# A diffusion-transformer block on one core: takes of k and loads of x tied to VectorE's place, one more tile normed in the projection, the last output tiles stored in quarters

## The chip, the core and the metric

The kernel runs on one core of a Trainium2 chip. The core has five engines that work beside each other, each with its own queue of instructions: TensorE (PE: matmuls; the loading of its weights is listed apart as PEld), VectorE (DVE), ScalarE (ACT), GpSimd (POOL) and SyncE (SP, here only a queue for data transfers). A transfer (DMA) is issued from the queue of SP, ACT or POOL and then moves data by itself. The engines wait for each other only through semaphores. The metric is the time of one execution in microseconds on the device; less is better.

## The reference

Two sequences of 2048 tokens with 576 features go through one transformer block whose norms are modulated by a condition:

```python
mod = silu(c) @ w_ada + b_ada
sh_msa, sc_msa, g_msa, sh_mlp, sc_mlp, g_mlp = split(mod, 6, axis=1)
xn = ln(x) * (1 + sc_msa) + sh_msa
q, k, v = split_heads(xn @ w_qkv + b_qkv)      # 16 heads of 36
q, k = ln(q) * qn_g + qn_b, ln(k) * kn_g + kn_b
o = softmax(q @ k.T * 36**-0.5) @ v
x = x + g_msa * (o @ w_proj + b_proj)
xn2 = ln(x) * (1 + sc_mlp) + sh_mlp
x = x + g_mlp * (gelu(xn2 @ w1 + b1) @ w2 + b2)   # 576 -> 2304 -> 576
```

All is in float32.

## The kernel before

The kernel first tests on the device whether the norms' gains and biases are small (then softmax needs no maximum) and branches. With the reference's inputs `block_of_small` runs, and the rest of this section is about it.

**Stages.** For each of the two sequences ("blocks", b = 0, 1): `inputs` norms 16 tiles of 128 tokens, multiplies them with w_qkv, norms the heads and lays q and k out by feature in two large tiles, qo (features 0 to 639) and kr (640 to 1151). `attend` then does the attention, and `outputs` the projection with the residual. After both blocks comes the MLP in two halves: the first product with GELU, whose results go to DRAM, and the second product, `second_product`, which reads them back for 256 tokens at a time (q = 0 to 15) and stores the output. Both halves of the MLP use Strassen's scheme with seven products in the place of eight.

**The attention.** The 16 heads are worked in 8 pairs p; each pair has 4 blocks qb of 512 queries, and each of these 4 groups g of keys. A step (p, qb, g) computes scores (L981), exponentials on ACT (L985) and, one step behind, the products with v (L994). DVE copies the first group's result into a tile ot (L1040) and adds the next three (L1042). There are two ot tiles. When the fourth group is in, `finish` sends the row of sums through DRAM to be spread over 64 partitions (den, L1009 and L1010), and three steps later `divided` takes the reciprocal, multiplies, and stores the result with SP's queue from ot into qo (L1019), where the q of the same pair lay. Only then is this ot tile free.

Scores need q and k at certain partitions. They are brought there by transfers within the on-chip memory: `take_q(p, qb)` brings 512 queries into qm (main dims) and qe (the last four dims of each head, four times), 8 to 10 transfers on SP's queue, asked for one qb ahead; `take_k(p)` brings all keys of a pair into km[p % 2] and ke[p % 2], 8 to 10 transfers on POOL's queue, asked for at step (p - 1, 1, 1). What a take returns (`parted`, on DVE) is run some steps later: the list `later` holds work by the number of steps that it is put off.

**The residual.** Beside the attention, `residual_begun(b, t)` prepares x + bias: it loads tile t of x into spare[t % 2], adds the bias to tile t - 1 on POOL, and stores it to x1_dram. The spare tiles lie in kr, in keys that are no longer needed. It is hooked to step (3 + t // 4, t % 4, 3), t = 0 to 16.

**What sets the order.** TensorE's instructions run in the order of the program throughout. In the attention, DVE's and POOL's do too (a manual schedule). A fixed order is not a fixed time: an engine runs ahead in its queue as far as its semaphores let it. POOL's instructions in the attention are takes of k and the residual; a take of k waits for nothing but the last scores that read its tile, those of the pair two before. ACT's and SP's order is set by the framework's planner, which also puts some later transfers of POOL (L1085, loads of x1 for the projection) among the attention's.

**The projection of block 1.** `outputs` calls `placed(t)` at each of 16 places t; `between` holds what is done there. For the MLP's first block of 512 tokens (four tiles i) it is: load the tile with ACT's queue (place 2i + 5), norm it (2i + 7, DVE with a square root on ACT), transpose it on TensorE and modulate it on ACT (2i + 8). In the MLP, `ahead(job)` does the same for the next block's tiles, with POOL's queue: load at a job three before, norm one before, four transposes (L1393) one behind and the fifth two behind. For tile (1, 0), which is wanted at the very start, the load stands before the first job and the norm in job 0. ACT's first instruction of the MLP is the copy of a product into cs (L1360). The rows' tiles xt go round: five of them in the attention and the projection, three in the MLP.

**The end.** In `second_product` the seven products come as pairs (3, 4), (2, 5), (6, 7) and (1,). DVE combines them into c00, c01, c10, c11, the quarters of y for two tiles of 128 tokens, multiplies by the gate (L1505), adds the residual xr (L1506), and POOL's queue stores each tile (L1507).

Of the kernel before, what the change touches and what calls it, by code (L numbers as in the profile page):

```python
# [8 lines left out]
F32 = mybir.dt.float32  # L9
# [3 lines left out]
ALU = mybir.AluOpType  # L13
# [3 lines left out]
P = 128  # L17
# [14 lines left out]
def dit_block(  # L32
# [25 lines left out]
    nc = tc.nc  # L58
# [6 lines left out]
    HALF = C // 2  # L65
    BLK = 512
    NBLK = N // BLK
    TPB = BLK // P
# [71 lines left out]
    with tc.tile_pool(name="bound", bufs=1, side="right") as bound:  # L140
# [11 lines left out]
        product = bound.tile([1, 1], F32, name="product")  # L152
# [129 lines left out]
    with psum_pools(), tc.tile_pool(name="ada", bufs=2) as ada:  # L282
# [11 lines left out]
        for i, ins in enumerate(((qn_g, kn_g), (qn_b, kn_b))):  # L294
# [3 lines left out]
            out=gb_rows, in_=rows_dram.rearrange("i w h d -> (i w h d)").rearrange("(c p) -> c p", p=P)  # L298
# [53 lines left out]
    def modulated(dst, src, which, b, apart=False):  # L352

        t4, t1 = transposed(*src, apart)
        for k in range(NKC):
            nc.scalar.activation(  # L356
                dst[:, k, :],
                t4[:, k * P : (k + 1) * P] if k < FULL else t1[:, :P],
                AF.Identity,
                bias=mod[:, which, k, b : b + 1],  # L360
                scale=mod[:, which + 1, k, b : b + 1],
            )
# [353 lines left out]
    def block_of_small():  # L716
# [13 lines left out]
        kv, close_kv = opened("kv")  # L730
# [9 lines left out]
        for t in (*ke, *qe):  # L740
            nc.gpsimd.memset(t, 0.0)
        high = kv.tile([P, BLK], F32R, name="high")

        low_k, low_q, sign_k, sign_q = (kv.tile([P, 1], F32, name=f"part{i}") for i in range(4))
        parts = ident.rearrange("p (r a b) -> p r a b", a=2, b=2)
# [35 lines left out]

        def take_k(p):
            m, e = km[p % 2], ke[p % 2]
            src = lambda c: slice(c * N // 2, (c + 1) * N // 2)
            rows_taken(nc.gpsimd, m, e, range(2), C + p * 2 * HD, src, slice(0, N // 2))
            return lambda: parted(e, slice(0, P), low_k, sign_k)
# [39 lines left out]
        def tile_normed(xt):  # L826
            return rows_normed(xs["pool"], xt)
# [235 lines left out]
        spare = [kr[:, c, a * 640 : a * 640 + C] for c in range(4) for a in range(3)]  # L1063

        def residual_begun(b, t):

            if t == 0:
                nc.gpsimd.dma_start(out=spare[2], in_=gate_dram[1, b, :].partition_broadcast(P))
            if t < NT:
                nc.gpsimd.dma_start(out=spare[t % 2], in_=x[b, t * P : (t + 1) * P, :])  # L1070
            if t > 0:
                rows = spare[(t - 1) % 2]
                nc.gpsimd.tensor_tensor(rows, rows, spare[2], ALU.add)
                nc.gpsimd.dma_start(out=x1_dram[b, (t - 1) * P : t * P, :], in_=rows)
# [160 lines left out]
        NB = B * NBLK  # L1235
        NPART = BLK // PAIR
        gelus = [dram.tile([NPART, P, NF, PAIR], F32, name=f"gelu{n}") for n in range(NB)]
        mx, close_mx = opened("mx")
        xnts = [mx.tile([P, NKC, BLK], F32, name=f"xnt{i}") for i in range(2)]
# [22 lines left out]
        def mlp_loaded(n, i, queue):  # L1262
            b, blk = divmod(n, NBLK)
            t0 = blk * BLK + i * P
            return tile_loaded(x1_dram[b, t0 : t0 + P, :], queue)

        first, between = {}, {}
        for i in range(TPB):
            cols = slice(i * P, (i + 1) * P)
            between.setdefault(2 * i + 8, []).append(  # L1270
                lambda i=i, cols=cols: modulated(xnts[0][:, :, cols], first[i], 2, 0)
            )
            between.setdefault(2 * i + 5, []).append(lambda i=i: first.update({i: mlp_loaded(0, i, nc.scalar)}))
            between.setdefault(2 * i + 7, []).append(lambda i=i: first.update({i: tile_normed(first[i])}))
        for i, t in enumerate((6, 8, 10, 12, 14)):
            between.setdefault(t, []).append(weight_sums[i])
        in_order = tc.manual_schedule(engines={mybir.EngineType.DVE})
# [97 lines left out]
        def ahead(job):  # L1375


            n, f = divmod(job, HF)

            def at(offset):  # L1380
                m, g = divmod(job - offset, HF)
                return (m + 1, g // 2) if m + 1 < NB and g % 2 == 0 and g // 2 < TPB else None

            if todo := at(-3):
                rows_ahead[todo] = mlp_loaded(*todo, nc.gpsimd)
            if todo := (1, 0) if job == 0 else at(-1):
                rows_ahead[todo] = tile_normed(rows_ahead[todo])
            for offset, chunks in ((1, range(FULL)), (2, (FULL,))):
                if todo := at(offset):
                    m, i = todo  # L1390
                    src, tail = rows_ahead[todo] if offset == 1 else rows_ahead.pop(todo)
                    for k in chunks:
                        nc.tensor.transpose(  # L1393
                            ps_t[:, k % FULL * P : (k % FULL + 1) * P],
                            src[:, k * P : (k + 1) * P] if k < FULL else tail,
                            ident,
                        )
                    for k in chunks:
                        nc.scalar.activation(
                            xnts[m % 2][:, k, i * P : (i + 1) * P],  # L1400
                            ps_t[:, k % FULL * P : (k % FULL + 1) * P],
                            AF.Identity,
                            bias=mod[:, 2, k, m // NBLK : m // NBLK + 1],
                            scale=mod[:, 3, k, m // NBLK : m // NBLK + 1],
                        )
# [14 lines left out]
            nc.sync.dma_start(out=hidden[q % len(hidden)], in_=gelus[n][g])  # L1420

        rows_ahead = {}
        for i in range(2):
            rows_ahead[1, i] = mlp_loaded(1, i, nc.gpsimd)
        token_sums(0)
        for job in range(0, NB * HF, 2):
            (n0, f0), (n1, f1) = divmod(job, HF), divmod(job + 1, HF)
# [26 lines left out]
        def second_product(q, gate, gate_bias):  # L1454

            b, t0 = divmod(q * PAIR, N)
            ht = hidden[q % len(hidden)]

            def part(t, k):
                return ht[:, k * HF : (k + 1) * HF, t * P : (t + 1) * P]  # L1460

            stationary = {3: part(0, 0), 4: part(1, 1)}
            for m, x_, y_, op in (
                (2, part(1, 0), part(1, 1), ALU.add),
                (5, part(0, 0), part(0, 1), ALU.add),
                (6, part(1, 0), part(0, 0), ALU.subtract),
                (7, part(0, 1), part(1, 1), ALU.subtract),
                (1, part(0, 0), part(1, 1), ALU.add),
            ):
                stationary[m] = hs.tile([P, HF, P], F32, name=f"as{m}")  # L1470
                nc.vector.tensor_tensor(stationary[m], x_, y_, op)  # L1471
            xr = []
            for t in range(2):
                xr.append(hs.tile([P, C], F32, name="xr", bufs=2))
                nc.sync.dma_start(out=xr[t], in_=x1_dram[b, t0 + t * P : t0 + (t + 1) * P, :])
                nc.gpsimd.tensor_tensor(xr[t], xr[t], gate_bias, ALU.add)
            y = [hs.tile([P, 2, HALF], F32, name="y", bufs=3) for _ in range(2)]
            c00, c01, c10, c11 = y[0][:, 0, :], y[0][:, 1, :], y[1][:, 0, :], y[1][:, 1, :]
            ms = {}
            for pair in ((3, 4), (2, 5), (6, 7), (1,)):  # L1480
                ps = s_tile()
                for a, m in enumerate(pair):
                    ms[m] = ps[:, a, :HALF]
                    for f in range(HF):
                        nc.tensor.matmul(  # L1485
                            ms[m], stationary[m][:, f, :], ws[m][:, f, :], start=(f == 0), stop=(f == HF - 1)
                        )
                if pair == (3, 4):
                    nc.vector.tensor_copy(c01, ms[3])
                    nc.vector.tensor_copy(c10, ms[4])  # L1490
                elif pair == (2, 5):
                    nc.vector.tensor_tensor(c00, c10, ms[5], ALU.subtract)
                    nc.vector.tensor_tensor(c11, c01, ms[2], ALU.subtract)
                    nc.vector.tensor_tensor(c10, c10, ms[2], ALU.add)
                    nc.vector.tensor_tensor(c01, c01, ms[5], ALU.add)
                elif pair == (6, 7):
                    nc.vector.tensor_tensor(c11, c11, ms[6], ALU.add)
                    nc.vector.tensor_tensor(c00, c00, ms[7], ALU.add)
            if q + 3 < NB * NPART:
                hidden_loaded(q + 3)  # L1500
            nc.vector.tensor_tensor(c00, ms[1], c00, ALU.add)
            nc.vector.tensor_tensor(c11, ms[1], c11, ALU.add)
            for t in range(2):
                rows = y[t].rearrange("p a f -> p (a f)")
                nc.vector.tensor_tensor(rows, rows, gate, ALU.mult)  # L1505
                nc.vector.tensor_tensor(rows, rows, xr[t], ALU.add)  # L1506
                nc.gpsimd.dma_start(out=out[b, t0 + t * P : t0 + (t + 1) * P, :], in_=rows)  # L1507
# [49 lines left out]
```

## Time and profile before

| | |
|---|---|
| median of 3 runs | 3247.49 us (3244.83 to 3251.32) |
| the profiled execution | 3251.16 us, of which the span from the first to the last instruction is 3249.3 us |
| TensorE's granted clock | 0.997 of full speed |

Stages by the trace, with the busy time of the engines in them:

| stage | from | to | PE | DVE | ACT | POOL |
|---|---|---|---|---|---|---|
| attention, block 0 | 256 | 1050 | 791.80 | 287.15 | 534.15 | 84.85 |
| projection, block 0 | 1050 | 1122 | 71.59 | 26.50 | 1.86 | 10.28 |
| inputs, block 1 | 1122 | 1366 | 244.00 | 159.06 | 81.50 | 33.77 |
| attention, block 1 | 1366 | 2140 | 772.49 | 270.18 | 529.59 | 74.84 |
| projection, block 1 | 2140 | 2214 | 74.00 | 42.58 | 9.59 | 17.14 |
| MLP, first product | 2214 | 2746 | 529.14 | 259.80 | 256.82 | 14.54 |
| MLP, second product | 2746 | 3235 | 489.00 | 244.79 | 1.77 | 78.04 |
| end | 3235 | 3250 | 0.04 | 3.67 | 0.00 | 1.10 |

How to read the profile's lines: L12 is line 12 of the kernel, `out<-in` are tiles by their names in the program, `xN` is how many instructions are merged in a row. A timeline row has start and duration in microseconds, the instruction, and in brackets how long its engine had been idle and what ended that. A chain row has start, duration and what the end of the kernel was waiting for at that time. A q behind an engine's name (SPq) means its sequencer, which waits, branches and issues. An instruction that issues a transfer is listed with the time of the issue; the data land later.

### The profile page before, as it was taken

Reading aid. Unit: us, or ns where it says so; the run is one execution under the profiler, and the core shown is the slowest. Engines: PE = TensorE matmul, PEld = TensorE weight load, DVE = VectorE, ACT = ScalarE, POOL = GpSimd, SP = SyncE. Lnnn points to the kernel's source line nnn. Section 1 sums busy time; section 2 is a strip of 40 time slices with the busy share of each in tenths; the row PEclk is TensorE's granted clock in tenths of the full one; section 3 lists DMA queues with packets and bytes.
Section 4 is the critical chain, followed back from the end, with each engine's and each line's share of the span. In section 5 each row is a group of like instructions: output and inputs, shape, how many; then the busy total and the mean of one; then the engine's idle time right before and its main releaser. Section 6 shows DMA issues by size and latency. Waiting matters only on the chain.

```text
span 3249.3 us, 46887 instructions
## 1 busy us (share of the span) xinstructions
PE 3212.6 (99%) x18143; PEld 1884.8 (58%) x18143; DVE 1450.2 (45%) x2073; ACT 1496.4 (46%) x2950; POOL 354.1 (11%) x435
## 2 busy tenths in 40 slices
PE   8999999999999999999999999999999999999998
PEld 5775333333333777633333333367888888777776
DVE  4664333333333366633333333345555443455454
ACT  2335666666666033366666666623555542000000
POOL 1111000012200111100011110010000000111111
PEclk9999999999999999999999999999999999999999
DMA  4112222233311411121223222154322223333321
GB/s 130 26 25 65 76 51 61 74 77 85 93 33 34 144 26 27 25 54 44 51 71 75 59 55 66 33 181 149 119 90 94 87 84 127 135 125 113 116 99 38
DMA packets 127795, 253.15 MB, mean 78 GB/s; under 512 B 22915, under 2 KB 65868, under 8 KB 125516
## 3 DMA queue, kind: packets, MB, share of 16 engines
q1 hardware_dynamic: 103956, 181.48, 18.3%
q0 software_dynamic: 22880, 67.11, 7.5%
q8 instruction: 145, 2.38, 0.3%
q10 hardware_dynamic: 728, 1.48, 0.2%
q14 instruction: 86, 0.70, 0.1%
HBM read 135.40 MB, written 66.35 MB: 62 GB/s over the span
## 4 chain that ended last, share of the span: by engine, by line
PE 95%; issue 2%; DMA 1%; DVE 1%; POOL 0%; SPq 0%; ACT 0%; DVEq 0%; POOLq 0%; ACTq 0%
PE b L994 28%; PE b L981 19%; PE s L370 14%; PE s L1485 14%; PE m L1334 12%; PE m L1348 2%; PE s L381 2%; PE one L1334 2%; PE s L884 1%; PE t L1393 0%; PE s L348 0%; DMA wq<-in_w_qkv_dram 0%; DMA qo<-ot 0%; DMA wa<-in_w_ada_dram 0%; PE b L192 0%
## 5 line engine op out<-in xcount | busy, mean ns | idle before, releaser
L985 ACT ACTIVATE pt<-b 128x512 f32<-128x512 f32 x2048 | 1058.0, 608 | 493.4 <-PE b L994 276.8
L994 PE MATMUL b<-pt,vt 128*64 128x512 f32 x4096 | 936.7, 599 | 0.0
L994 PEld LDWEIGHTS b<-pt,vt 128*64 128x64 f32 x4096 | 272.1, 137 | 582.8 <-issue 441.3
L981 PE MATMUL b<-qm,km 32*128 32x512 f32 x4096 | 570.7, 614 | 3.3 <-DVE ot L1040 2.5
L981 PE MATMUL b<-qe,ke 16*128 16x512 f32 x2048 | 424.3, 788 | 0.0
L1042 DVE TENSOR_TENSOR ot<-b,ot 128x512 f32<-128x512 f32 x192 | 132.8, 692 | 650.3 <-PE b L994 649.8
L370 PE MATMUL s<-wq,xnt 128*128 128x288 f32 x1536 | 392.8, 411 | 1.6 <-DMA wq<-in_w_qkv_dram 1.6
L981 PEld LDWEIGHTS b<-qm,km 32*128 32x128 f32 x4096 | 192.8, 185 | 275.5 <-ACT pt L985 206.9
L1485 PE MATMUL s<-ws,as 128*128 128x288 f32 x1440 | 351.8, 406 | 0.0
L370 PEld LDWEIGHTS s<-wq,xnt 128*128 128x128 f32 x1536 | 286.3, 191 | 93.3 <-issue 18.5
L1485 PEld LDWEIGHTS s<-ws,as 128*128 128x128 f32 x1440 | 273.6, 190 | 75.6
L1013 DVE RECIPROCAL den<-den 128x512 f32<-128x512 f32 x64 | 214.0, 3343 | 11.7 <-DMA den<-den_dram 11.7
L1334 PE MATMUL m<-xnt,wb 128*128 128x256 f32 x864 | 214.0, 384 | 0.0
L1334 PE MATMUL m<-s,wb 128*128 128x256 f32 x864 | 210.1, 379 | 0.2 <-DVE s L1304 0.2
L1040 DVE COPY ot<-b 128x512 f32<-128x512 f32 x64 | 44.3, 692 | 343.7 <-PE b L994 315.7
L1334 PEld LDWEIGHTS m<-xnt,wb 128*128 128x128 f32 x864 | 159.2, 190 | 32.5 <-issue 12.2
L1334 PEld LDWEIGHTS m<-s,wb 128*128 128x128 f32 x864 | 164.1, 190 | 22.9 <-DVE s L1304 0.6
L981 PEld LDWEIGHTS b<-qe,ke 16*128 16x128 f32 x2048 | 108.7, 184 | 114.7 <-issue 113.0
L1361 DVE TENSOR_TENSOR cs<-m,cs 128x512 f32<-128x512 f32 x72 | 49.7, 691 | 215.6 <-ACT cs L1360 154.0
L1485 PE MATMUL s<-ws,hidden 128*128 128x288 f32 x576 | 142.3, 406 | 0.0
L356 ACT ACTIVATE xnt<-s,mod 128x128 f32<-128x128 f32 x180 | 66.8, 460 | 160.2 <-PE s L349 146.3
L1471 DVE TENSOR_TENSOR as<-hidden 128x1152 f32<-128x1152 f32 x80 | 139.0, 1801 | 0.0
(162 smaller groups left out, 2550.0 us busy)
## 6 DMA issues: line engine op xcount, KB each, us to landing
gelu<-cs SPq DMA_DIRECT2D x144, 256.0 KB
hidden<-gelu SPq DMA_DIRECT2D x16, 2304.0 KB
den<-den_dram SPq DMA_DIRECT2D x128, 128.0 KB
x_dram<-kr POOLq DMA_DIRECT2D x48, 288.0 KB, 3.3
qm<-qo SPq DMA_DIRECT2D x192, 64.0 KB
kr<-in_x_dram POOLq DMA_DIRECT2D x32, 288.0 KB, 3.8
xr<-x_dram SPq DMA_DIRECT2D x32, 288.0 KB
out_dram<-y POOLq DMA_DIRECT2D x32, 288.0 KB, 3.8
```

The source lines that it names most:

```text
L356: nc.scalar.activation(dst[:, k, :], t4[:, k * P : (k + 1) * P] if k < FULL else t1[:, :P], AF.Identity, bias=mod[:, which, k, b : b + 1], ...
L370: nc.tensor.matmul(outs[a], stationary(k, a), moving(k, a), start=(first and k == 0), stop=(not first and k == FULL - 1),)
L381: nc.tensor.matmul(outs[a], stationary(FULL, a)[r], moving(FULL, a)[r], start=first, stop=not first)
L981: nc.tensor.matmul(ps, k[r, keys], q[r, :], start=first, stop=not first)
L985: nc.scalar.activation(pt[:, h, :], banks[2 * c + h], AF.Exp, scale=SCALE)
L994: nc.tensor.matmul(acc[64 * h : 64 * h + 64, :], vt[:, v0 : v0 + 64], pt[:, h, :], start=pt is pts[0][0], stop=pt is pts[-1][0],)
L1013: nc.vector.reciprocal(den, den)
L1042: nc.vector.tensor_tensor(ot, acc, ot, ALU.add)
L1334: nc.tensor.matmul(out_m[m], wb[:, slot[m], k, f * P : (f + 1) * P], moving[m](k), start=k == 0 and (m == 1 or (first and m in (2, 5, 6))) ...
L1348: nc.tensor.matmul(out_m[m], w[r, f * P : (f + 1) * P], a[r, FULL, t * PAIR : (t + 1) * PAIR], start=first and m != 4, stop=not first and ...
L1471: nc.vector.tensor_tensor(stationary[m], x_, y_, op)
L1485: nc.tensor.matmul(ms[m], stationary[m][:, f, :], ws[m][:, f, :], start=(f == 0), stop=(f == HF - 1))
```

## The change

Three parts. First, a helper `not_sooner(tile)` copies one element of a tile on DVE. It stands ahead of the transfers of `take_k(p)` for p > 2 (one copy for each of the two tiles) and ahead of each load of x in `residual_begun`. A transfer that overwrites the element must come after the copy, and DVE comes to the copy in the order of the program; so POOL can't issue these transfers before DVE has reached this place.

Second, the work on tile (1, 0), the first of the MLP's second block, moves from the MLP's start into block 1's projection, so that five tiles are loaded, normed and modulated there. All places of these five are two earlier than before. In the MLP, its load, its norm in job 0 and its transposes in jobs 1 and 2 are gone.

Third, in the last call of `second_product`, each quarter of the output is multiplied by the gate and given the residual as soon as its sums are complete but for the last product, and is stored by itself with SP's queue: two quarters behind pair (2, 5), and two at the end, where the last product is multiplied by the gate (in the tile xr, which is free by then) and added.

```diff
+        met = kv.tile([1, 1], F32, name="met")
+        def not_sooner(there):
+            nc.vector.tensor_copy(met, there[0:1, 0:1])
...
         def take_k(p):
             m, e = km[p % 2], ke[p % 2]
+            if p > 2:
+                not_sooner(m)
+                not_sooner(e)
...
             if t < NT:
+                not_sooner(spare[t % 2])
                 nc.gpsimd.dma_start(out=spare[t % 2], in_=x[b, t * P : (t + 1) * P, :])
...
-        for i in range(TPB):
-            cols = slice(i * P, (i + 1) * P)
-            between.setdefault(2 * i + 8, []).append(
-                lambda i=i, cols=cols: modulated(xnts[0][:, :, cols], first[i], 2, 0)
+        for j in range(TPB + 1):
+            n, i = divmod(j, TPB)
+            to = xnts[n][:, :, i * P : (i + 1) * P]
+            between.setdefault(2 * j + 6, []).append(lambda j=j, to=to: modulated(to, first[j], 2, 0))
+            between.setdefault(2 * j + 3, []).append(
+                lambda j=j, n=n, i=i: first.update({j: mlp_loaded(n, i, nc.scalar)})
             )
-            between.setdefault(2 * i + 5, []).append(lambda i=i: first.update({i: mlp_loaded(0, i, nc.scalar)}))
-            between.setdefault(2 * i + 7, []).append(lambda i=i: first.update({i: tile_normed(first[i])}))
+            between.setdefault(2 * j + 5, []).append(lambda j=j: first.update({j: tile_normed(first[j])}))
...
-                return (m + 1, g // 2) if m + 1 < NB and g % 2 == 0 and g // 2 < TPB else None
+                there = m + 1 < NB and g % 2 == 0 and g // 2 < TPB and (m, g) > (0, 0)
+                return (m + 1, g // 2) if there else None
...
-            if todo := (1, 0) if job == 0 else at(-1):
+            if todo := at(-1):
...
-        for i in range(2):
-            rows_ahead[1, i] = mlp_loaded(1, i, nc.gpsimd)
+        rows_ahead[1, 1] = mlp_loaded(1, 1, nc.gpsimd)
...
+            last = q == NB * NPART - 1
...
+            def half_stored(t, n):
+                nc.sync.dma_start(out=half(out[b, t0 + t * P : t0 + (t + 1) * P, :], n), in_=y[t][:, n, :])
...
+                if last and len(pair) == 2 and pair != (3, 4):
+                    for t in range(2):
+                        n = 1 - t if pair == (2, 5) else t
+                        part = y[t][:, n, :]
+                        nc.vector.tensor_tensor(part, part, half(gate, n), ALU.mult)
+                        nc.vector.tensor_tensor(part, part, half(xr[t], n), ALU.add)
+                        if pair == (2, 5):
+                            half_stored(t, n)
+            if last:
+                for t in range(2):
+                    product = half(xr[t], t)
+                    nc.vector.tensor_tensor(product, ms[1], half(gate, t), ALU.mult)
+                    nc.vector.tensor_tensor(y[t][:, t, :], y[t][:, t, :], product, ALU.add)
+                    half_stored(t, t)
+                return
```

More of the change, by code (lines that the diff above doesn't have):

```diff
@@ L1479, in second_product, with half @@
             ms = {}
+            def half(ap, n):
+                return ap[:, n * HALF : (n + 1) * HALF]
+            def half_stored(t, n):
+                nc.sync.dma_start(out=half(out[b, t0 + t * P : t0 + (t + 1) * P, :], n), in_=y[t][:, n, :])
             for pair in ((3, 4), (2, 5), (6, 7), (1,)):
```

## The prediction

> **What bounds the kernel now.** I read the page from the top: first the engines' busy shares, then the chain that ended last, then the list of waits of TensorE, and last the stretches where one of these waits sits.
>
> ```profile
> PE 3212.6 (99%) x18143; PEld 1884.8 (58%) x18143; DVE 1450.2 (45%) x2073; ACT 1496.4 (46%) x2950; POOL 354.1 (11%) x435
> ...
> PE 95%; issue 2%; DMA 1%; DVE 1%; POOL 0%; SPq 0%; ACT 0%; DVEq 0%; POOLq 0%; ACTq 0%
> ```
>
> TensorE is busy 99% of the span and is 95% of the chain. The change takes no matmul away, so it can gain only where TensorE stands still, and at the ends of the kernel. Its waits in the middle are few:
>
> ```profile
> PE t L1393 <- DVE xt L278: 2.7, 1, 2.7
> PE b L981 <- DVE ot L1040: 2.5, 2, 1.4
> ```
>
> The columns are microseconds in total, times, longest. The second row understates the loss, because a late start also spreads the matmuls behind it. I therefore take the distance between the starts of successive L994 runs (one step of attention each) from the chain of waits around the wait in pair 3 of block 0:
>
> ```profile
> 566.52 3.58 PE b L994 x16
> ...
> 572.50 1.03 PE b L994 x4
> ...
> 574.97 3.78 DMA qo<-ot
> ...
> 580.97 3.58 PE b L994 x16
> ...
> 586.95 3.58 PE b L994 x16
> ```
>
> A step takes 5.98 us (572.50 - 566.52; 586.95 - 580.97), and the stalled one 8.47: lost 2.49. The same chain around 1663 in block 1 has starts at 1657.08, 1663.06, 1671.30, 1678.97: 2.26 + 1.69 lost. Two more lost steps are in block 0, 766.38 to 773.02 (0.66) and 862.70 to 869.12 (0.44). All four places end with DVE's copy of a sum into ot (L1040) waiting for the store qo<-ot that still reads that buffer. **Sum 7.5 us.**
>
> Why is that store late? It stands on SyncE's queue behind the takes of q. In the timeline of SyncE's queue, the stalled place and then the next, undisturbed one:
>
> ```profile
> 560.32 4.75 SPq L764 DMA_DIRECT2D qm<-qo  x4
> 565.12 6.28 SPq L767 DMA_DIRECT2D qe<-qo  x3
> 571.45 1.83 SPq L764 DMA_DIRECT2D qm<-qo  x2
> 573.38 0.67 SPq L767 DMA_DIRECT2D qe<-qo  x1
> 574.15 1.56 SPq L1019 DMA_DIRECT2D qo<-ot  x2
> ...
> 586.73 2.84 SPq L764 DMA_DIRECT2D qm<-qo  x4
> ```
>
> Ten takes need 13.7 us (560.32 to 574.05) where they need 7.7 at 586.73 (to 594.40). Beside the first ones run the eight takes of k, which POOL issued from 560.58 on, when TensorE ended the pair before: its queue runs ahead to the start of every pair, where SyncE is busiest.
>
> **The change, part by part.**
>
> *Ties (take_k of pairs 3 to 7, residual_begun).* Added are 5 x 2 x 2 + 16 x 2 = 52 copies of one element on DVE. No such row exists; the nearest, the reciprocal of 128x1 (L277), takes 0.16 us: 8.3 us in all, on an engine that is busy 287 of 794 us in the first attention, so nothing on the path. What they wait for: k's main and end tiles were written a whole pair earlier; the residual's tile was last written by POOL's addition one hook earlier, some 24 us (four steps) before. So I cost the wait at 0. If POOL came later than that, behind the copy stand the sums into ot, and TensorE waits for these.
>
> The takes of k now start behind DVE's sum of step (p, 1, 0). In the undisturbed place that sum is at 596.55 to 597.24, while the takes of q ended at 594.40 and the qo<-ot store was issued by 596.83. So the eight takes (4.5 us of POOL's issue, 0.5 to 0.6 each, 6.3 us to landing) run from about 597.5 to 609, and the next takes of q start at 610.64. Beside them is only the exchange of the sums (den), whose reader, the reciprocal, comes three steps (18 us) later. The parting of k on DVE stands four steps (24 us) behind, against 11 us for the takes. Hidden. At pair starts the takes of q then need their 5.4 or 7.5 us, and the store comes 4 us before its reader (its last packet in the trace at 598.2, L1040 at 602.53). Gain: the whole **7.5 us**; ends: 0 if the takes stay slow, and a loss in the rival below.
>
> The residual's load and store (288 KB each) move from bursts at pair starts to one pair at each fourth step, about 4.5 us behind the start of a take of q. [...] The POOL addition now lies beside DVE's reciprocal; at 783.23 they lay together and it took its usual 3.34.
>
> *Tile (1, 0) normed in the projection.* Moved are one load (from POOL, 0.54, to ACT's queue, 0.33 to 0.36), one norm (DVE 2.2 from 2173.22 to 2175.41, ACT 0.5), five transposes (0.66 + 0.27 of PE, equal before and after) and five modulations (ACT 1.86). The chain of waits at the start of the MLP shows what goes:
>
> ```profile
> 2221.94 0.04 ACT cs L1360
> ...
> 2222.74 0.59 DVE xt L278
> ...
> 2223.37 0.66 PE t L1393 x4
> ```
>
> ACT was held at its copy cs (L1360) until 2221.94 and its sqrt stood behind, so TensorE waited 2.7 us for the norm. Without these transposes its next work (L1348, 3.4 us, then some 7 us) needs nothing of ACT; the sums of DVE that free the bank end near 2226.5, TensorE needs the bank near 2231. Late next is nothing. In the projection all norms come two places earlier. The new first one meets DVE idle (6.39 us before 2167.04) and ends near 2162, 6 us before TensorE wants it at 2168.4. The load's data are block 0's, written long before; the other four loads were issued at 1282.9 to 1325.5, the fifth follows tile 15's transposes near 1345, where ACT has 0.9 us idle. **-2.7 us**, ends 0 and -3.0.
>
> *The last tiles.* The last matmul ends near 3235.1. Behind it now come two additions, four operations of 576 columns and POOL's stores:
>
> ```profile
> 3235.08 0.46 DVE L1501 TENSOR_TENSOR y<-s,y 128x288 f32<-128x288 f32 x1 [3.55 <-PE s L1485]
> ...
> 3239.26 0.55 POOL L1507 DMA_DIRECT2D out_dram<-y  x1 [0.98 <-DVE y L1506]
> ```
>
> The program's last line, by engine and kind (count, ns min/median/max, first and last start):
>
> ```profile
> L1553 SPq EVENT_SEMAPHORE  x14: 17/28/28, 3212.2 to 3249.2; - x14
> ...
> L1553 POOLq DRAIN  x3: 46/98/6514, 3241.9 to 3249.0; - x3
> ```
>
> POOL's drain begins at 3241.9, before the last store landed (3242.06), and lasts 6.51 us; the span ends 0.8 us behind it. So not the store, but POOL's drain sets the end. In the change POOL's last work is the addition to xr, which ended at 3214.7, so its drain can lie beside the matmuls. Then the end is: four DVE operations of 288 columns (0.46 + 0.53 + 0.37 + 0.45, with 0.1 for the wait between dependent ones): 3237.0; SyncE's issue 0.36: 3237.4; its branch to the last line, 3.4 us (before: branch 3208.8, first wait 3212.2); ten waits of 0.06; the closing 0.8: about 3242.2. That is **-7.1 us**. The four new operations behind each of the pairs (2, 5) and (6, 7), 4 x 0.37 = 1.5 us, lie beside 8.7 and 4.4 us of matmuls.
>
> [...] The drain's price in the new place no row shows. Ends: if it always follows the last store, only the earlier issue is won (3239.8 to 3237.4, -2.4); if free, -7.1. I take -7.1, since ACT's drain (2755.7) and PE's (3234.0) ran as soon as these engines were through.
>
> **Sum:** 7.5 + 2.7 + 7.1 = 17.3. The profiled execution took 3251.16 (span 3249.3), so it would be 3233.9; the median of the runs shown is 3247.49 (3244.83 to 3251.32), 3.7 below: **3230**.
>
> **Rivals.**
> A. The drain stays at the end: 17.3 - 4.7 = 12.6, 3235. For it: the drain outlasts the last landing by 6.4. Against: it didn't wait to begin.
> B. The takes of q stay slow at pair starts (then k's takes were not the cause), attention keeps its 7.5: 9.8, 3238. Against: 7.3 to 7.7 in every undisturbed place. That the tie does not hold POOL back ends here too.
> C. Both: 5.1, 3242.
> D. Slower: k's takes and the residual now press on the qo<-ot store, which is in flight just when they start. It has 4.3 us from last packet to reader; once its landing (1.4 us beside nothing, 3.0 beside the residual at 575.7) passes 5.7, L1040 waits and TensorE with it. At the price of the stall of pair 3, 2.5 us, at ten places (pairs 2 to 6, two blocks): +25 against 9.8 won, about 3263. For it: k's takes nearly doubled the takes of q. Against: their first packets come 1 us after the issue, when the store is mostly through.
>
> **Chances:** forecast 0.60 (its own range 3225 to 3234), A 0.11, B 0.07, C 0.09, D 0.13. No change is within 0.2%, 6.5 us, about what a measurement can tell. Faster: forecast, A, B: 0.78. Same: C: 0.09. Slower: D: 0.13. The range, 3225 to 3243, takes in A to C and leaves D out.
>
> **What would show it.** Right: no L1040 waiting for qo<-ot; ten takes in 7 to 8 us at every pair start; POOL's km rows of pairs 3 to 7 some 37 us later in the pair; no row L1393 <- DVE; POOL's drain before 3225, the end some 7 us behind the last matmul. Wrong: DVE copies that wait for POOL, L994 steps over 6 us at (p, 1, 0) (D), a 6.5 us drain at the end (A).

## The result and the profile after

| | before | after |
|---|---|---|
| median | 3247.49 us (3244.83 to 3251.32) | 3231.15 us (3230.51 to 3231.41) |
| profiled execution | 3251.16, span 3249.3 | 3230.51, span 3228.7 |

The ratio of the times is 0.9950, interval 0.9935 to 0.9964: 16.3 us less by the medians, where 17.3 were forecast, and 20.6 us less between the two profiled spans. The kernel has also become steadier: its runs lie within 0.9 us of each other, those of before within 6.5. In all that follows, a time is compared with that of the kernel before in the same session (3247.5 to 3249.2).

Line numbers of after are higher by 6 to 35: L990 are the scores, L1003 the products with v, L1049 and L1051 the copy and the sums into ot, L770 and L773 the takes, L1028 the store qo<-ot. The busy shares, the shares of the chain that ended last, and the list of TensorE's waits on the page and trace of after:

```profile
PE 3206.4 (99%) x18143; PEld 1883.0 (58%) x18143; DVE 1450.4 (45%) x2131; ACT 1495.7 (46%) x2950; POOL 353.5 (11%) x432
...
PE 99%; DMA 1%; DVE 0%; SPq 0%; issue 0%; ACT 0%; DVEq 0%
```

```profile
PE s L370 <- DMA wq<-in_w_qkv_dram: 2.5, 1, 2.5
PE s L370 <- DVE ot L1051: 0.8, 1, 0.8
...
PE m L1345 <- DVE s L1315: 0.2, 1, 0.2
```

TensorE's share of the chain went from 95% to 99%. Neither the 2.7 us for the norm in the MLP nor a wait for ot's copy is left among its waits; those shown, and one of 10.6 us for the first weights, are what remains to gain on the other engines' side. Note PE's busy time: it fell by 6.2 us though the count of matmuls is the same. That is the hint to look for matmuls that had run slowly.

By stages (from the starts of the first matmuls of each; the rest is equal to 0.2 us):

| stage | before | after | difference | forecast |
|---|---|---|---|---|
| ahead of the first product | 22.94 | 22.22 | -0.7 | 0 |
| attention, block 0 | 784.47 | 781.00 | -3.5 | -3.6 |
| attention, block 1 | 776.62 | 772.56 | -4.1 | -3.95 |
| projection, block 1 | 73.63 | 74.14 | +0.5 | |
| MLP, first product | 531.96 | 526.89 | -5.1 | -2.7, with the row above |
| behind the last matmul | 14.65 | 6.92 | -7.7 | -7.1 |

SyncE's queue at the place where the forecast began, the start of pair 3 (timeline of after):

```profile
559.53 2.83 SPq L770 DMA_DIRECT2D qm<-qo  x4
562.42 2.14 SPq L773 DMA_DIRECT2D qe<-qo  x3
564.60 1.49 SPq L770 DMA_DIRECT2D qm<-qo  x2
566.19 0.68 SPq L773 DMA_DIRECT2D qe<-qo  x1
568.11 1.56 SPq L1028 DMA_DIRECT2D qo<-ot  x2
```

Ten takes of q now need 7.3 us (559.53 to 566.87) instead of 13.7, and the store follows six us earlier. The takes of k are elsewhere (timeline of POOL in after):

```profile
588.37 0.55 POOL L1080 DMA_DIRECT2D kr<-in_x_dram  x1 [84.45 <-DVE met L747]
594.64 0.51 POOL L770 DMA_DIRECT2D km<-kr  x1 [5.72 <-PE b L990]
...
598.60 0.58 POOL L773 DMA_DIRECT2D ke<-kr  x1
```

They began at 560.58 before; the first row's bracket shows the tie at work, POOL's queue held 84 us by the copy met. The copies themselves take 0.13 to 0.14 us each and none waited for another engine.

The end (timeline of after, then the program's last line by engine and kind):

```profile
3222.25 0.46 DVE L1530 TENSOR_TENSOR xr<-s,gate 128x288 f32<-128x288 f32 x1 [1.70 <-PE s L1504]
...
3223.60 0.46 DVE L1531 TENSOR_TENSOR y<-y,xr 128x288 f32<-128x288 f32 x1
```

```profile
L1588 SPq EVENT_SEMAPHORE  x14: 17/28/28, 3227.1 to 3228.7; - x14
L1588 POOLq DRAIN  x3: 46/98/6269, 3203.3 to 3228.4; - x3
```

DVE's part is 1.81 us as forecast. POOL's drain of 6.27 us runs from 3203.3, beside matmuls, and SyncE's arrival at the last line (3227.1) is the last thing waited for. From the first of these additions to the end are 6.5 us.

### The profile page after: what moved, and what is told of

It reads as the page before. It is cut to its first block, busy times and chain, and to the rows that moved or that the text cites. A ratio compares the mean times of both kernels' runs of the same rounds, so it can differ in the third digit from the quotient of the medians.

```text
span 3228.7 us, 46962 instructions
## 1 busy us (share of the span) xinstructions
PE 3206.4 (99%) x18143; PEld 1883.0 (58%) x18143; DVE 1450.4 (45%) x2131; ACT 1495.7 (46%) x2950; POOL 353.5 (11%) x432
## 4 chain that ended last, share of the span: by engine, by line
PE 99%; DMA 1%; DVE 0%; SPq 0%; issue 0%; ACT 0%; DVEq 0%
PE b L1003 28%; PE b L990 19%; PE s L370 16%; PE s L1504 15%; PE m L1345 12%; PE s L381 2%; PE m L1359 2%; PE one L1345 2%; PE s L893 1%; PE s L348 1%; PE t L1405 0%; DMA wq<-in_w_qkv_dram 0%; PE b L192 0%; DMA wa<-in_w_ada_dram 0%; PE b L893 0%; PE s L349 0%
## 5 line engine op out<-in xcount | busy, mean ns | idle before, releaser
L1003 PE MATMUL b<-pt,vt 128*64 128x512 f32 x4096 | 935.0, 598 | 0.0
L1003 PEld LDWEIGHTS b<-pt,vt 128*64 128x64 f32 x4096 | 271.8, 136 | 582.0 <-issue 439.4
L990 PE MATMUL b<-qm,km 32*128 32x512 f32 x4096 | 567.5, 614 | 0.3 <-DVE vt L945 0.3
L1051 DVE TENSOR_TENSOR ot<-b,ot 128x512 f32<-128x512 f32 x192 | 132.7, 691 | 653.1 <-PE b L1003 652.6
L990 PE MATMUL b<-qe,ke 16*128 16x512 f32 x2048 | 423.2, 790 | 0.0
L990 PEld LDWEIGHTS b<-qm,km 32*128 32x128 f32 x4096 | 192.0, 184 | 270.1 <-ACT pt L994 206.5
L1049 DVE COPY ot<-b 128x512 f32<-128x512 f32 x64 | 44.2, 691 | 334.7 <-PE b L1003 334.7
L990 PEld LDWEIGHTS b<-qe,ke 16*128 16x128 f32 x2048 | 108.4, 184 | 114.2 <-issue 112.6
```

The costliest lines, as they stand in the source:

```text
L990: nc.tensor.matmul(ps, k[r, keys], q[r, :], start=first, stop=not first)
L1003: nc.tensor.matmul(acc[64 * h : 64 * h + 64, :], vt[:, v0 : v0 + 64], pt[:, h, :], start=pt is pts[0][0], stop=pt is pts[-1][0],)
L1051: nc.vector.tensor_tensor(ot, acc, ot, ALU.add)
```

## The experiments

**Each part alone.** Theory: three independent gains that add up. e1_ties is before with `not_sooner` for k and for the residual, e2_tile before with tile (1, 0) moved, e3_tail before with the quarters; each takes its hunks of the diff as they stand.

> Before plus the ties alone (takes of k of pairs 3 to 7 and the residual's loads). Theory: the stalls come from takes of k that lie beside takes of q; the attention loses its five late steps, 7.5 us, so about 3240; the MLP's 2.7 us wait for the norm and a POOL drain of 6.5 us at the end stay. Rival: the ties gain nothing by themselves (the stalls come from elsewhere), 3247. Rival: the 52 DVE copies wait for POOL and hold TensorE, over 3250.

> Before plus the tile (1, 0) normed in the projection alone. Theory now: the stall of 2.7 us also puts TensorE's granted clock to a half for 3.4 us behind it, which costs another 1.4 to 1.7, so about -4.4 us, 3243, with no clock record under full speed near the MLP's start; the stalls in the attention stay. Rival: only the wait itself goes, -2.7 us, 3245, and the MLP's first jobs take as long as before.

> Before plus the quarters on SP's queue alone. Theory: POOL's drain of 6.5 us moves beside the matmuls, the end is 6.9 us behind the last matmul instead of 14.7, so -7.1 to -7.7 us, 3240. Rival (A): the drain stays at the end, -2.4 us, 3245.

| | median | difference | ratio |
|---|---|---|---|
| e1_ties | 3242.69 | -6.5 | 0.9982 (0.9973 to 0.9991) |
| e2_tile | 3244.95 | -4.2 | 0.9993 (0.9984 to 1.0002) |
| e3_tail | 3242.23 | -6.9 | 0.9983 (0.9974 to 0.9992) |

Together 17.6 by the medians, against 16.3 of the change. By the ratios, which use the same runs, the parts sum to about 0.42% (13.6 us) against 0.50%: they add up within the noise, no closer. The interval of e2_tile takes in no change, so no gain in its time is shown; its profile does show the MLP's first product 5.07 us shorter and the projection 0.50 longer. In the profile of e3_tail the end is 7.08 us. In e1_ties no step of the attention is late, and both the stall in the MLP and the drain at the end remain.

What e1_ties can bring differs from run to run, because the late steps do. The lost time in four profiled executions without ties is 7.5 (before), 5.1 (e2_tile), 4.0 (e3_tail) and 3.8 (e8_whole_sync). So the profile of before had a large loss, and a median can gain less than this profile. The tied kernels have none of it.

**Which tie does it.** Theory: the takes of k slow the takes of q, and the residual has no part in the loss. e4_takes is before with the ties of k alone, e7_resid before with those of the residual alone; e12_no_resid is after without the latter:

```diff
             if t < NT:
-                not_sooner(spare[t % 2])
```

> Before plus the ties of the takes of k alone; the residual's loads and stores still run ahead to the next take of k. Theory: the takes of k are what slows the takes of q, so most of the 7.5 us goes: ten takes of q in 7 to 8 us at pair starts, 3240 to 3242. Rival: the bursts of the residual slow them as much: half or less of the gain, 3244 to 3247.

> Before plus the ties of the residual's loads alone. The takes of k of pairs 4 to 7 stand behind a tied load in POOL's fixed order, so they too leave the pair's start (only the take for pair 3 doesn't). Theory: the five late steps go as with the ties of the takes, 3241 to 3243. Rival (only a tie at the take itself helps): 3247 to 3249.

> After without the residual's ties (those of the takes of k stay). Theory: the takes' ties bring the whole gain of the attention and the residual's bring none: 3231, the same as the change. Rival: the residual's bursts make a step late now and then: a median of 3232 to 3234 and a wider spread than the 1 us of the change.

e4_takes: 3242.00, -7.2 (ratio 0.9983, 0.9974 to 0.9992), no late steps. e12_no_resid: 3231.27, -17.6 (0.9946, 0.9932 to 0.9960), the same as the change. So the ties of k bring the attention's gain by themselves, and those of the residual nothing that can be measured.

e7_resid fell out otherwise than expected: 3257.32, **8.6 us slower** than before (1.0025, 1.0016 to 1.0035). Its profile shows why. POOL, SyncE and DVE in pair 3 of e7_resid, from three timelines:

```profile
591.03 0.55 POOL L1077 DMA_DIRECT2D kr<-in_x_dram  x1 [122.69 <-DVE met L747]
591.58 0.51 POOL L770 DMA_DIRECT2D km<-kr  x1
```

```profile
594.75 5.34 SPq L1025 DMA_DIRECT2D qo<-ot  x2
```

```profile
603.94 0.69 DVE L1046 COPY ot<-b 128x512 f32<-128x512 f32 x1 [7.26 <-DMA qo<-ot]
```

POOL works in a fixed order. The tied load of x holds its queue for 123 us, and the untied takes of k, which stand behind it, start when it is let go: 591.58, 5.7 us earlier in the pair than in after (594.64; e7's pair 3 begins 2.66 us later, at 562.19). There they meet the store qo<-ot, whose two issues take 5.34 us instead of 1.56, and DVE's copy waits for it. It happens again in other pairs: nine steps of 7.2 to 10.0 us instead of 5.98. Not all of that is waiting: the trace grants half the clock for 13.7 us in e7's attentions (the first stretch follows the stall shown), worth about 6.8 us by an estimate that takes TensorE as busy throughout. This is rival D's mechanism at another place: the takes of k press on the store, not on the takes of q.

**How near that is in the change.** Theory of the forecast: the place (p, 1, 1) lies just in a gap. Rivals: any quiet place would do; or the store is pressed there too. e6_takes_at_store asks for the takes one step earlier, e5_takes_at_q two steps, where takes of q begin:

```diff
-                if g == 1 and qb == 1 and p + 1 < NPAIR:
+                if p is not None and (qb, g) == ((1, 0) if p > 1 else (1, 1)) and p + 1 < NPAIR:
```

(e5 has `(0, 3)` in the place of `(1, 0)`.)

> After, but the tied takes of k are asked for at (p, 1, 0): DVE comes to them when SyncE issues the store of ot. Theory: the store has 4 us from its last packet to its reader and takes of k slow it by some 2 us, so nothing is late, 3231, the store only lands later. Rival D of the prediction: the store lands more than 4 us later, L1040's place waits at up to ten places, up to 2.5 us each, 3240 to 3255.

> After, but the tied takes of k of pairs 3 to 7 are asked for at step (p, 0, 3) instead of (p, 1, 1): DVE then comes to them just as SyncE begins the takes of q for (p, 2). Theory (takes of k beside takes of q make the stores of ot late): the takes of q at these ten places need 9 to 14 us instead of 5.4 to 7.5, L994 steps over 6 us come back behind them, most at pair 3, in sum 3 to 8 us: 3234 to 3239. Rival (what hurt was POOL's burst of takes and residuals together, or the pair's start itself): no late step, 3231.

e6_takes_at_store: 3235.60, -13.1 (0.9957, 0.9941 to 0.9974), so 3 to 4 us of the gain are lost again. Four steps are late, 6.35 to 7.45 us. At one of them, POOL's timeline and two pieces of the chain of waits of e6:

```profile
881.04 0.52 POOL L770 DMA_DIRECT2D km<-kr  x1 [1.51 <-PE b L1003]
```

```profile
882.06 7.21 DMA qo<-ot
...
889.35 0.70 DVE ot L1049
```

The takes start 1.7 us before the store's second issue (882.78), and the chain waits 7.2 us for the store. In after, at the same place, the takes start at 881.93, behind the store's last issue (it ended at 881.70), and DVE's copy at 886.56 waited for TensorE alone. In pair 3 of e6 they start 0.2 us before the second issue and no step is late. So the takes can come 0.2 us before it and not 1.7; in after they come 1.0 us behind it, and the copy on DVE is in the right place by some 1 to 3 us.

e5_takes_at_q: 3262.96, slower than before by 14.2 (1.0041, 1.0027 to 1.0055) and than the change by some 30, where a few microseconds were expected. Most of that is not the collision meant to be tested. The parting of k (L783, L784) is put off four steps from the take, so it had moved too, into the step of the reciprocal (timeline of DVE in e5):

```profile
615.04 0.69 DVE L1051 TENSOR_TENSOR ot<-b,ot 128x512 f32<-128x512 f32 x1 [4.11 <-PE b L1003]
...
616.21 2.40 DVE L784 SCALAR_TENSOR_TENSOR ke<-ke,part,high 128x512 fp32r<-128x512 f32 x1
...
619.83 3.35 DVE L1022 RECIPROCAL den<-den 128x512 f32<-128x512 f32 x1
...
623.82 0.68 DVE L1051 TENSOR_TENSOR ot<-b,ot 128x512 f32<-128x512 f32 x1
```

DVE has 8.8 us of work between two sums that should be 6 apart, and TensorE waits for the second. e9_takes_q_only therefore moves the takes as e5 does and leaves the parting where it was:

```diff
-            behind, later = None, [[] for _ in range(5)]
+            behind, later = None, [[] for _ in range(7)]
...
-                    later[4].append(take_k(p + 1))
+                    later[6 if p > 1 else 4].append(take_k(p + 1))
```

> As the run with the takes of k asked for at (p, 0, 3), but k's parting on DVE stays at its old place (two more steps behind the take), so that only the place of the transfers differs from the change. Theory: the takes of q at the ten places need 9 to 13 us, the stores behind them are late at pairs 3 and 5 (ten takes) and hardly at 2, 4 and 6 (eight), 2 to 7 us in sum: 3233 to 3238; the 32 us of the earlier run were DVE's pile-up, not the transfers. Rival: the transfers alone cost the 32 us, 3260.

e9_takes_q_only: 3233.27 (0.9952, 0.9937 to 0.9967), 2.0 us over e12_no_resid of the same session. Its two attentions are 1.7 us longer than after's; those of e5 were 37.6 us longer in the profile, so nearly all of e5's loss comes with the parting. Part of it is again the clock: half of full speed for 27.3 us in e5's attentions and at no time in e9's, by the same estimate 13.7 of the 37.6 us. In e9 the takes of q need 12.9 us in pair 3 and 8.6 to 10.5 elsewhere: slowed as forecast, with only three steps late, by 0.2 to 1.0. The takes' collision alone is thus cheaper than the profile of before suggests. What else the late steps of before need (the residual's store in flight beside qo<-ot, the half clock told of below) is read from its trace alone; no run takes one of these away at the pair's start.

**The end.** Theory: POOL's drain takes its time behind whatever POOL did last, and set the end. Rival: the whole tiles' stores did. e8_whole_sync is before with its last two whole tiles stored from SyncE's queue; e10_quarters_pool is after with the quarters on POOL's queue; e11_pool_last is after with one more write of POOL behind DVE's last addition, into a tile that nothing reads afterwards:

```diff
e8:
-                nc.gpsimd.dma_start(out=out[b, t0 + t * P : t0 + (t + 1) * P, :], in_=rows)
+                queue = nc.sync if q == NB * NPART - 1 else nc.gpsimd
+                queue.dma_start(out=out[b, t0 + t * P : t0 + (t + 1) * P, :], in_=rows)
e10, in half_stored:
-                nc.sync.dma_start(...)
+                nc.gpsimd.dma_start(...)
e11, behind the last addition:
+                nc.gpsimd.memset(half(xr[1], 1), 0.0)
```

> Before, but the last two output tiles are stored whole from SP's queue instead of POOL's; no quarters. Theory: the end is POOL's drain, so the queue alone brings most of the tail's gain: SP's last issue near 3239.5, its branch 3.4 us, 0.7 of waits and 0.8 to close, the end some 5 us earlier, 3243. The quarters themselves are worth the other 2 us. Rival: the quarters bring the gain and the queue nothing, 3248.

> After, but the four quarters are stored from POOL's queue. Theory: POOL's drain needs some 6.3 us whenever POOL comes to it, so it stands at the end again: POOL's last issue near 2.3 us behind the last matmul, 2.7 to its last line, 6.3 to 6.5, 0.8 to close: some 5.5 us more than the change, 3237. Rival: the quarters made the gain, 3231 to 3232.

> After, with one memset of 128x288 on POOL put behind the very last DVE operation (it clears a part of xr that nobody reads any more); no transfer of POOL's is under way then. Theory: the drain's 6.3 us are fixed, whatever POOL did last: 3236 to 3238. Rival: the drain waits for POOL's transfers and is short without them: 3231 to 3232.

e8_whole_sync: 3242.17, -6.6 (0.9980, 0.9971 to 0.9990); in its profile the end is 9.47 us, so of the 7.6 that e3_tail saves there, 5.2 come from the queue and 2.4 from the quarters. e10: 3237.24 (0.9963, 0.9949 to 0.9976) and e11: 3236.14 (0.9960, 0.9945 to 0.9975), which is 6.0 and 4.9 us over e12_no_resid. In the last line of e11:

```profile
L1589 POOLq DRAIN  x3: 46/98/6269, 3229.6 to 3236.5; - x3
```

The first start is that of the long drain: it lasts 6.269 us behind a short write, to the nanosecond what it lasts in after, with no transfer of POOL under way. In e10 it lasts 6.597 behind a store. In e8_whole_sync and e3_tail, where it begins beside matmuls, it lasts 6.352 and 6.401. So the stores account for little of it: 6.3 to 6.6 us are paid in every profile read, once when POOL is through, and they cost no time when POOL is through early.

None of these kernels is measurably faster than the change.

## Why the prediction was right, point by point

**Attention, 7.5.** 7.53 in the profiled execution, by the mechanism that was named. The k takes' new place at (p, 1, 1) holds: no copy of a sum waits for the store, and e6 shows that this was close. The cost 0 for 52 copies stands, and for the residual's new place, for which the forecast's sum counts nothing, no loss shows either (e12 against the change). In before, one stretch had ten takes of q beside two stores and a load of the residual (timelines of SyncE and POOL):

```profile
778.78 2.98 SPq L764 DMA_DIRECT2D qm<-qo  x4
781.81 1.39 SPq L767 DMA_DIRECT2D qe<-qo  x2
...
785.37 0.66 SPq L767 DMA_DIRECT2D qe<-qo  x1
```

```profile
780.09 0.56 POOL L1074 DMA_DIRECT2D x_dram<-kr  x1 [0.30 <-POOL kr L1073]
782.82 0.55 POOL L1070 DMA_DIRECT2D kr<-in_x_dram  x1 [2.17 <-DMA x_dram<-kr]
...
785.09 0.56 POOL L1074 DMA_DIRECT2D x_dram<-kr  x1 [0.30 <-POOL kr L1073]
```

They took 7.3 us (778.78 to 786.03), against 7.7 at the undisturbed place of 586.73. As a forecast for the median the term is a draw from losses of 3.8 to 7.5, which the one profile couldn't show.

**MLP's start, 2.7.** The mechanism is right, the size isn't: with the projection's +0.5 the profile gained 4.6. The term left out lies behind the stall. L1348 in before and L1359 in after are the same 16 matmuls (timelines, before first):

```profile
2223.96 3.45 PE L1348 MATMUL m<-xnt,wr 64*128 64x256 f32 x16
```

```profile
2212.88 2.00 PE L1359 MATMUL m<-xnt,wr 64*128 64x256 f32 x16
```

3.45 us against 2.00. I had read 3.4 as their duration. The windows of before (length, busy time and count of PE, PEld, DVE, ACT and POOL, granted clock, DMA share, GB/s) and the same place in e4_takes, which has the same stall:

```profile
2221.00:2224.00 3.00, 0.63 (x6) 0.46 (x6) 1.43 (x4) 0.81 (x3) 0.00 (x0) 1.00 1.06 380
2224.00:2228.00 4.00, 4.00 (x19) 2.90 (x19) 3.16 (x8) 3.46 (x8) 0.00 (x0) 0.57 0.43 140
```

```profile
2216.00:2220.00 4.00, 4.00 (x28) 3.19 (x28) 3.38 (x9) 3.37 (x9) 0.00 (x0) 1.00 0.55 179
```

In before the clock granted behind the stall is half (0.57 in the mean of this window), 19 matmuls run where e4 has 28, and 1.7 us more are lost. Of six profiles with this stall three show it (before; e3_tail, where the mean of 2219 to 2224 is 0.66; e7_resid) and three don't (e1_ties; e4_takes, with 1.00 above; e8_whole_sync). The +1.69 of the step at 1671, which the forecast took from the chain without naming a cause, coincides with the same: the trace of before grants half the clock for 3.4 us from 1671.4 on, behind an idle time of TensorE of 1.14 us (row at 1669.94).

**The end, 7.1.** 7.7 in the profile; the difference is about SyncE's branch to the last line, 2.6 us where 3.4 were taken. The assumption that decided, that the drain does not wait for the end, is confirmed. Rival A priced a late drain at 4.7; e11 measured 4.9. For storing in quarters the forecast's sum counts no cost; no run times a quarter's store by itself, and with SyncE's queue in both the end is 2.4 us shorter with quarters (7.08 in e3_tail, 9.47 in e8_whole_sync).

**The sum.** 17.3 forecast against 20.6 in the profile (+1.9 in the MLP, +0.6 at the end, 0.7 ahead of the first product, which no part of the change explains) and 16.3 in the medians. That the median came out within 1.2 us of the forecast owes something to two errors that cancel: the MLP's term was too small for that profile, and the attention's too large for a median.

**Rivals.** A, B and C are out: the drain moved, and the takes of q recovered. D did not happen here, but its mechanism is real within 3 to 6 us of the chosen place (e6, e7), at 3 to 9 us of price rather than 25, since not every pair is hit.

## What to carry to other kernels

An order written in the program is not a time: a queue that waits for nothing can run ahead to the worst moment (the takes of k at 560.58 in before), and one tiny copy (0.13 us) on the engine that keeps the time can hold it, if it is put where nothing is in flight; two or three microseconds decided here. What is moved takes others along, the work tied to it (e5) and whatever stands behind it in a fixed order (e7), so move one thing at a time and look at both. At the end of a kernel ask which engine finishes last and what its own closing costs (POOL's 6.3 to 6.6 us here), before making the last transfers smaller.

## What the runs showed of the hardware that was not expected

- After idle times of TensorE of 1.14 and 2.67 us (both in before) the granted clock was 0.5 for 3.413 us, in some executions and not in others of the same stall: in e4_takes it stayed 1.00 behind 2.71 us. By the wait alone the MLP's stall would cost 2.7 us, in the profile it was 4.6. What decides whether the clock falls, no run shows.
- POOL's last drain takes 6.27 to 6.40 us where no store of its own has just been issued (after, e11, e8, e3), and 6.51 (before) and 6.60 (e10) behind its own stores.
- DVE's two-input L784 took 2.40 us instead of 0.75 beside a POOL addition of 1.42 us (e5), and a one-input L777 of before took 2.03 instead of 0.48, at 585.21, beside one of 1.41; the reciprocal, beside one too (at 783.23 in before, at 755.58 in after), kept its 3.3. Why, no run shows. The ties put POOL's additions beside the reciprocal and so, by chance, to a place where they did not slow it (3.33 to 3.35 us in all 64 of after); what that is worth was not measured.
